# A gated unit with a quantised second product: block 11 of the first batch moves to the seven-product scheme, in a new order of steps

## The chip, the core and the metric

The kernel runs on one core of one Trainium2 chip. The core has four compute engines, each with its own queue that it works off in order: TensorE (PE, matrix products; PEld is its weight load), VectorE (DVE), ScalarE (ACT) and GpSimd (POOL). SyncE (SP) computes nothing here; it issues the transfers between the chip's memory (DRAM) and the on-chip memory, and also waits for its next instruction's inputs in order. The results of TensorE go to banks of PSUM, where ScalarE and VectorE read them. The metric is the device time of one launch in microseconds (us); the time before is 719.89 us, the median of three runs from 719.88 to 720.88.

## The reference

Four sequences of 1024 tokens with 512 features. Each is normalised, scaled by a row that depends on a condition vector, and goes through a gated unit whose down weights and hidden values are quantised.

```python
scale = cond @ norm_w.T + 1.0
ms = jnp.mean(x * x, axis=-1, keepdims=True)
h = x * (scale[:, None, :] * jax.lax.rsqrt(ms + EPS))
u = h @ up_w.T                       # 512 -> 2 x 2048
val, gate = jnp.split(u, 2, axis=-1)
h = val * jax.nn.gelu(gate, approximate=False)
hq = act_quant(h)                    # per token, 127 steps
wq = weight_quant(down_w)            # -1, 0, 1 times one scale
y = hq @ wq.T
return y + x
```

## The kernel before

A batch is one sequence: two halves of 512 tokens. The 2048 hidden rows are 16 blocks of 128. The first matrix product is made in fp16 from a high and a low part of each operand. For one block there are two ways to make it.

**The plain way.** `half_gate` and `half_value` (through `plain`, whose matmuls are at L715) make gate and value of one half of the tokens, 12 matmuls each over 512 columns. A block takes four such products, 48 matmuls. `half_gelu` (ScalarE, L761) and `half_out` (VectorE, L771) follow for each half.

**The seven-product way.** A class `Slot` makes a block's two halves of tokens at once from sums and differences of quarters of the weights and of the tokens: seven products (`product`, L700) of six matmuls each. Its steps have numbers in the written order: 0 first product, 1 its copy to a second bank (ScalarE, L807), 2 fourth product, 3 its copy (ScalarE, L815), 4 fifth product, 5 its copy (ScalarE, L822), 6 second product, 7 its gelu (ScalarE, L829), 8 third product, 9 its output (VectorE, L835), 10 gate product, 11 a sum (VectorE, L843), 12 the second gelu (ScalarE, L846), 13 value product, 14 a sum (VectorE, L852), 15 the second output (VectorE, L855). Products 0, 4, 8 and 13 collect in one bank A, 6 in the bank B, 2 and 10 in one bank E. There are two banks A, one B and two E; the plain gates take A or B, the plain values E. A bank is taken again when what reads it has run.

Batches 1 to 3 use the seven-product way throughout, with weights that the first batch prepares and spills to DRAM (`s_dram`). In the first batch the blocks below `FAST` go the plain way and those from `FAST` on (12 to 15 before) the other one.

**What the first batch prepares for a block j.** `w_load` brings the weights (SyncE, L306), `w_range` takes the mean of their size on ScalarE (L322), `w_factor` makes a power of two of it (VectorE, L332 to L342), `w_scale` scales (ScalarE, L372). `rows_high` and `rows_low` split the rows into fp16 parts (ScalarE L398, VectorE L402), and `rows_turn` brings them, transposed by the transfer itself, to the place from which TensorE loads them (SyncE, L406). `s_sum` (L436), `s_high` (ScalarE, L453) and `s_low` (L457) make the sums of quarters; a third number 1 in the name of an s_sum, or of an s_low after the part's number, puts it on VectorE, else it runs on GpSimd. `s_spill` (SyncE, L469) stores the parts in DRAM for the later batches. For a block from `FAST` on, the first batch needs the sums itself: they are made in a tile `s_rows`, and `s_turn` (SyncE, L475) brings them transposed to the place that products 2, 4 (s_turn.j.0) and 10, 13 (s_turn.j.1) read; `rows_turn` then brings three parts of the rows and not four.

**The order.** The whole first batch after the first half block is one text, `FIRST_BATCH`, which `take` reads from left to right; each name is a step, with its block and its part. It fixes the order on every engine's queue and on that of SyncE. A step waits for what it reads and for the space that it writes, and everything behind it on its queue waits too. Steps on different queues that stand next to each other in the text need not run at the same time. Besides the steps above it holds the tokens of the second batch (`t_` steps; `t_turn` L675), the loads of the down weights (`d_` steps), the four turns of the first tokens (`turn`), the maxima for the quantisation (`max`, VectorE), and steps for the condition's rows (`c_`; `c_over`, `c_spread`, `c_rows` and `d_spread` have a small matmul each).

The batches after it have their own loops and their own planner (`Filler`), which the change does not touch.

Of the kernel before, what the change touches and what calls it, by code (L numbers as in the profile page):

```python
# [51 lines left out]
def glu_quant_kernel(  # L52
# [18 lines left out]
    NJ = FF // P  # L71
# [71 lines left out]
    FAST = NJ - 4  # L143
# [1216 lines left out]
    def take(steps):  # L1360
# [10 lines left out]
        w_scale.3.0 o_whole.1.0.1 out.1.0 gate.1.1 rows_high.3 rows_low.3 d_sum.4 w_load.5 gelu.0.1
        s_high.0.1 value.1.1 s_sum.1.1.1 s_high.1.0 s_low.0.1.1 s_spill.0.0 out.0.1 d_sum.5 w_factor.4
        s_sum.1.3.1 w_load.10 s_low.1.0.1 d_sum.6 gate.2.0 rows_turn.3 o_WHOLE.3.2.1 s_high.1.1 w_range.5
        s_low.1.1 w_scale.4.0 s_sum.2.0.1 value.2.0 s_sum.2.2.1 t_square.0.1 s_sum.2.3.1 w_factor.5 gelu.1.1
        o_sum.0 w_scale.4.1 s_spill.1.0 rows_high.4 out.1.1 d_load.0 c_over gate.2.1 s_spill.2.1 w_scale.5.0
        w_gain.2 o_sum.1 gelu.2.0 w_gain.4 o_sum.2 o_high.1 value.2.1 d_sum.7 out.2.0 s_sum.2.1.1 rows_low.4
        rows_turn.4 s_high.2.0 w_scale.5.1 s_low.2.0.1 gate.3.0 o_high.3 o_low.1 o_high.2 w_load.6 o_sum.3
        d_sum.2 value.3.0 o_low.3 rows_high.5 t_square.0.0 rows_low.5 rows_turn.5 gelu.2.1 gate.3.1 gelu.3.0
        out.2.1 gelu.3.1 out.3.0 c_range s_spill.2.0 w_load.9 value.3.1 o_low.2 w_load.7 s_spill.3.1
        w_range.6 w_load.11 s_sum.3.0.1 s_sum.3.2 d_load.1 s_high.2.1 w_factor.6 w_scale.6.1 t_root.0  # L1380
        c_spread c_rows gate.4.0 c_copy s_low.2.1.1 s_sum.3.3 w_scale.6.0 s_sum.3.1.1 out.3.1 rows_high.6
        rows_low.6 rows_turn.6 s_high.3.0 s_low.3.0 value.4.0 d_sum.3 max.0.0.0 w_range.7 max.1.0.0
        s_sum.4.0 gelu.4.0 gate.4.1 w_factor.7 o_high.0 s_sum.4.1 s_sum.4.2.1 s_spill.4.1 w_scale.7.0
        o_low.0 w_load.8 w_scale.7.1 c_store value.4.1 out.4.0 rows_high.7 max.1.0.1 s_high.3.1 rows_low.7
        rows_turn.7 d_sum.0 gate.5.0 s_high.4.0 s_low.4.0 s_low.3.1.1 max.0.1.0 d_sum.1 c_undo gelu.4.1
# [443 lines left out]
```

## Time and profile before

The profile is one execution on the chip. Times are in us from its first instruction; a busy time is the union of an engine's instructions.

| | |
|---|---|
| median of the runs shown | 719.89 us (719.88 to 720.88, three runs) |
| span of the profiled execution | 718.6 us (1.29 less than the median) |
| TensorE busy | 712.7 us, 3664 matmuls |
| VectorE, ScalarE, GpSimd busy | 587.3, 423.6, 135.9 us |
| the order's first matmul, block 11, slot 12, the second batch begin | 21.1, 132.4, 142.8, 176.5 us |

A row of a timeline gives the start, the length, the engine, the line, what is written and read, and the number of instructions merged. A row of groups gives the line, engine and operation, the count, the busy time in us, the mean of one in ns, and the idle time of the engine just before, with what ended it. A row of stretches gives the length, then each engine's busy time with its number of instructions (TensorE, weight loads, VectorE, ScalarE, GpSimd), the granted clock of TensorE, the mean busy share of the 16 DMA engines and the GB/s moved. The modelled end of a matmul overlaps the start of the next one; the start of one to that of the next is the pace.

### The profile page before, as it was taken

Reading aid. Unit: us, or ns where it says so; the run is one execution under the profiler, and the core shown is the slowest. Engines: PE = TensorE matmul, PEld = TensorE weight load, DVE = VectorE, ACT = ScalarE, POOL = GpSimd, SP = SyncE. Lnnn points to the kernel's source line nnn. Section 1 sums busy time; section 2 is a strip of 40 time slices with the busy share of each in tenths; the row PEclk is TensorE's granted clock in tenths of the full one; section 3 lists DMA queues with packets and bytes.
Section 4 is the critical chain, followed back from the end, with each engine's and each line's share of the span. In section 5 each row is a group of like instructions: output and inputs, shape, how many; then the busy total and the mean of one; then the engine's idle time right before and its main releaser. Section 6 shows DMA issues by size and latency. Waiting matters only on the chain.

```text
span 718.6 us, 10218 instructions
## 1 busy us (share of the span) xinstructions
PE 712.7 (99%) x3664; PEld 359.6 (50%) x3664; DVE 587.3 (82%) x880; ACT 423.6 (59%) x703; POOL 135.9 (19%) x143
## 2 busy tenths in 40 slices
PE   8999999999999999999999999999999999999998
PEld 4544444444444446665444445665444444445854
DVE  7898897889898879896788868876688888755896
ACT  6998865786568784544335676544334665333463
POOL 1703233330100215340100031460020000000120
DMA  7799988998985556777745547775945444443253
GB/s 255 255 273 299 259 211 242 261 226 210 252 207 118 130 160 140 217 173 172 152 100 116 132 100 195 162 181 160 203 105 102 102 102 102 100 95 99 104 171 122
DMA packets 227060, 121.57 MB, mean 169 GB/s; under 512 B 188969, under 2 KB 198461, under 8 KB 227010
## 3 DMA queue, kind: packets, MB, share of 16 engines
q1 hardware_dynamic: 226858, 120.80, 67.6%
q8 instruction: 28, 0.46, 0.3%
q14 instruction: 22, 0.18, 0.1%
q10 hardware_dynamic: 152, 0.13, 0.1%
HBM read 52.71 MB, written 23.09 MB: 105 GB/s over the span
## 4 chain that ended last, share of the span: by engine, by line
PE 99%; ACT 0%; DVE 0%; issue 0%
PE A L700 37%; PE E L700 19%; PE B L700 9%; PE po L1064 9%; PE pg L715 8%; PE pv L715 8%; PE po_end L1016 4%; PE pz L1181 1%; PE ptx L1165 1%; PE pv L786 0%; PE po_B L1064 0%; PE pg L786 0%; PE pw L382 0%; PE po_E L1064 0%; PE po_A L1064 0%; PE pc L211 0%
## 5 line engine op out<-in xcount | busy, mean ns | idle before, releaser
L700 PEld LDWEIGHTS <-SXY 128*128 128x128 f16 x2100 | 205.5, 98 | 240.5
L700 PE MATMUL A<-R,SXY 128*128 128x512 f16 x1146 | 264.8, 379 | 0.0
L700 PE MATMUL E<-R,SXY 128*128 128x512 f16 x582 | 141.5, 379 | 0.0
L835 DVE SCALAR_TENSOR_TENSOR H<-A,sg,t 128x512 f32<-128x512 f32 x52 | 39.0, 750 | 69.6 <-PE A L700 69.4
L987 DVE TENSOR_TENSOR H<-H,am 128x1024 f32<-128x1024 f32 x64 | 76.0, 1214 | 0.0
L846 ACT ACTIVATE t<-t,sg 128x512 f32<-128x512 f32 x52 | 37.5, 720 | 63.3 <-DVE t L843 63.3
L700 PE MATMUL B<-R,SXY 128*128 128x512 f16 x300 | 72.9, 379 | 0.0
L906 DVE TENSOR_REDUCE gm<-H 128x512 f32<-128x1024 f32 x56 | 69.1, 1233 | 1.0
L829 ACT ACTIVATE t<-B,sg 128x512 f32<-128x512 f32 x52 | 35.7, 687 | 37.8 <-PE B L700 37.8
L922 POOL PARTITION_ALL_REDUCE am<-R x8 | 14.3, 1793 | 229.6 <-DVE R L908 229.6
L715 PEld LDWEIGHTS <-SXY 128*128 128x128 f16 x342 | 33.4, 98 | 40.3 <-DVE SXY L424 0.4
L1064 PE MATMUL po<-wd,R 128*128 128x256 fp8e4 x416 | 52.4, 273 | 0.0
L822 ACT COPY t<-A 128x512 f32<-128x512 f32 x52 | 30.2, 580 | 37.5 <-PE A L700 37.1
L815 ACT COPY v<-E 128x512 f32<-128x512 f32 x52 | 30.4, 585 | 32.1 <-PE E L700 30.2
L1064 PEld LDWEIGHTS <-R 128*128 128x128 bf16 (+1 forms) x448 | 43.8, 98 | 8.9
L807 ACT COPY B<-A 128x512 f32<-128x512 f32 x52 | 29.7, 572 | 31.2 <-PE A L700 30.6
L855 DVE SCALAR_TENSOR_TENSOR H<-v,sg,t 128x512 f32<-128x512 f32 x52 | 40.8, 785 | 6.6 <-ACT t L846 6.6
L852 DVE TENSOR_TENSOR v<-A,v 128x512 f32<-128x512 f32 x52 | 35.6, 685 | 9.2 <-PE A L700 8.0
L995 ACT ACTIVATE H<-H 128x1024 f32<-128x1024 f32 x38 | 39.9, 1050 | 5.2 <-DVE H L987 5.2
L715 PE MATMUL pg<-R,SXY 128*128 128x512 f16 x180 | 41.4, 379 | 0.0
L908 DVE TENSOR_TENSOR R<-R,gm 128x512 f32<-128x512 f32 x56 | 40.3, 720 | 1.1
L999 ACT ACTIVATE R<-H 128x1024 bf16<-128x1024 f32 x38 | 40.1, 1056 | 1.0
(236 smaller groups left out, 947.3 us busy)
## 6 DMA issues: line engine op xcount, KB each, us to landing
SXY<-s_dram SPq DMA_DIRECT2D x46, 256.0 KB, 3.1
H<-in_L_cond_up_w_dram SPq DMA_DIRECT2D x13, 512.0 KB, 3.9
SXY<-s_dram SPq DMA_DIRECT2D x46, 128.0 KB, 3.4
s_dram<-SXY SPq DMA_DIRECT2D x15, 384.0 KB, 4.9
xr<-in_x_dram SPq DMA_DIRECT2D x19, 256.0 KB, 3.0
out_dram<-xr SPq DMA_DIRECT2D x19, 256.0 KB, 2.6
H<-in_x_dram SPq DMA_DIRECT2D x8, 512.0 KB, 7.7
R<-in_L_cond_down_w_dram SPq DMA_DIRECT2D x8, 512.0 KB
```

The lines of the kernel that those rows point to most:

```text
L700: PE.matmul(o, s[:, w, k, :], operand(g // NJ, c, l, k), start=start and n == 0, stop=stop and n == len(TERMS) - 1, skip_group_check=True,)
L715: PE.matmul(ps, a[k // 2][:, w, k % 2, :], XP[:, l, k, h * TOK : (h + 1) * TOK], start=n == 0, stop=n == len(terms) - 1,)
L829: ACT.activation(self.t1, self.B, AF.Gelu, scale=gain(self.g, 1))
L835: DVE.scalar_tensor_tensor(h_half(self.g, 0), self.A, gain(self.g, 0), self.t1, ALU.mult, ALU.mult)
L846: ACT.activation(self.t2, self.t2, AF.Gelu, scale=gain(self.g, 1))
L855: DVE.scalar_tensor_tensor(h_half(self.g, 1), self.v, gain(self.g, 0), self.t2, ALU.mult, ALU.mult)
L906: DVE.tensor_reduce(gm[0], v, AX.X, ALU.max, apply_absolute_value=True)
L908: return [largest, lambda: DVE.tensor_tensor(m, m, gm[0], ALU.max)]
L987: DVE.tensor_tensor(v, v, r.to_broadcast([P, 2, TOK]), ALU.mult)
L995: ACT.activation(v, v, AF.Copy, bias=MAGIC)
L999: ACT.activation(q, by_tile(v), AF.Copy, bias=-MAGIC)
L1064: PE.matmul(po, w[:, j], m, start=start and j == 0, stop=stop and j == n - 1, skip_group_check=True,)
```

## The change

`FAST` goes from 12 to 11, so block 11 gets the steps of a slot: `gate.11`, `value.11`, `gelu.11` and `out.11` (two each) leave the order, and `slot.11.0` to `slot.11.15`, `s_turn.11.0` and `s_turn.11.1` come in. Its sums are made in `s_rows` (two and two parts, not three and one) and spilled from there, and its rows are split and turned in three parts.

The order as a whole is written anew. The set of steps is otherwise the same, but for the engine of s_sum, s_low and t_sum steps: of the 64 s_sum, 36 stay on VectorE though not the same ones; of the 32 s_low, 11 are on VectorE after 20; of the 16 t_sum, 8 after 11. TensorE's products of the plain blocks change places in a few spots (gate.4.0 ahead of gate.3.1, gate.5.1 ahead of gate.5.0, gate.9.1 ahead of gate.9.0, gate.10.1 ahead of value.10.0).

The core of the diff, with the stretches that matter below:

```diff
@@ -140,7 +140,7 @@
     A21 = R[:, 0, 6144 : 6144 + 768].bitcast(F16).rearrange("p (n w f) -> p n w f", n=3, w=2)

-    FAST = NJ - 4
+    FAST = NJ - 5
...
@@ -1363,75 +1363,73 @@
     FIRST_BATCH = """
-        w_load.3 d_load.2 t_load.0 d_load.6 d_load.4 s_sum.0.1 o_whole.0.0.0 gate.1.0 x_scale.6 w_range.3
-        x_scale.7 gelu.1.0 o_whole.2.2.0 turn.4 w_range.2 turn.5 w_load.4 turn.6 turn.7 d_load.7 x_high.0
...
-        s_spill.5.2 out.6.0 rows_turn.10 t_square.1.1 gate.8.0 max.2.0.0 rows_high.11 t_root.1 gelu.7.1
-        s_sum.8.0.1 s_high.7.1 s_sum.8.2.1 s_spill.6.2 s_high.8.0 s_low.7.1.1 s_sum.8.3 s_spill.6.0
...
-        rows_high.12 t_low.1.0 t_turn.1.0 gelu.9.1 gate.10.0 rows_low.12 t_high.1.1 t_square.2.0 t_low.1.1
-        s_high.10.1 s_sum.11.1.1 rows_turn.12 s_sum.11.2.1 s_high.11.0 s_low.10.1 value.10.0 out.9.1
-        s_sum.11.3 gelu.10.0 t_turn.1.1 w_range.13 max.3.0.1 w_load.14 s_low.11.0.1 s_sum.12.1 t_square.2.1
-        s_spill.12.1 gate.10.1 w_factor.13 w_scale.13.1 out.10.0 s_high.11.1 s_spill.10.1 t_root.2
-        s_low.11.1.1 w_scale.13.0 s_spill.11.0 rows_high.13 value.10.1 t_scale.2.1 w_range.14 s_sum.12.0.1
-        s_sum.12.2.1 s_sum.12.3.1 w_load.15 s_high.12.0 rows_low.13 s_high.12.1 gate.11.0 rows_turn.13
-        gelu.10.1 s_low.12.0.1 s_sum.13.0 t_high.2.1 w_factor.14 out.10.1 s_spill.12.0 t_scale.2.0
-        t_high.2.0 t_sum.2.1 value.11.0 s_turn.12.0 max.2.1.0 w_scale.14.0 s_sum.13.2 gelu.11.0 s_low.12.1.1
-        w_scale.14.1 t_sum.2.0 out.11.0 gate.11.1 s_turn.12.1 gelu.11.1 s_sum.13.1 s_spill.12.2 s_spill.10.0
-        t_sum.2.2.1 t_load.3 s_sum.13.3 value.11.1 rows_high.14 rows_low.14 s_high.13.0 s_low.13.0.1
-        slot.12.0 slot.12.1 t_sum.2.3.1 s_spill.13.0 max.2.1.1 s_turn.13.0 slot.12.2 s_sum.14.0.1 t_high.2.2
-        t_low.2.2 rows_turn.14 slot.12.4 s_high.13.1 s_low.13.1 slot.12.3 slot.12.6 slot.12.5 max.3.1.0
-        w_range.15 slot.12.13 t_low.2.0 s_spill.13.2 w_gain.14 s_turn.13.1 s_sum.14.2.1 t_square.3.1
-        out.11.1 slot.13.0 s_high.14.0 s_sum.14.3 slot.12.14 t_turn.2.0 slot.12.7 w_factor.15 s_sum.14.1
-        slot.13.2 slot.13.1 s_low.14.0.1 t_square.3.0 s_spill.14.0 slot.13.6 w_scale.15.0 t_root.3
...
+        s_sum.0.1 w_load.3 d_load.2 x_scale.7 x_scale.6 gate.1.0 w_range.2 turn.7 turn.4 turn.6 turn.5 w_range.3
+        w_factor.3 w_factor.2 d_load.4 value.1.0 gelu.1.0 d_load.5 x_high.1 o_whole.0.0.0 x_high.2 x_high.0
+        s_sum.0.0.1 x_low.2 x_low.0 d_load.6 x_low.1 d_load.7 x_high.3 o_whole.2.2.0 s_sum.0.2 x_low.3 s_sum.0.3
+        w_scale.3.0 s_high.0.1 w_scale.2.1 gate.0.1 w_scale.2.0 s_high.0.0 s_low.0.0 w_load.4 rows_high.2
+        rows_low.2 s_sum.1.0.1 gelu.0.1 w_scale.3.1 rows_high.3 t_load.0 d_sum.4 d_load.3 c_largest rows_turn.2
...
+        w_factor.11 gate.8.0 s_low.7.0 out.7.0 s_sum.7.3 t_low.0.1 t_square.1.1 s_high.7.1 s_sum.8.1.1
+        s_sum.8.0.1 s_spill.6.0 s_spill.9.1 out.6.0 s_spill.5.2 s_sum.8.2.1 w_scale.11.1 s_low.7.1 s_high.8.0
+        w_scale.11.0 s_sum.8.3 s_low.8.0.1 s_sum.9.1 rows_high.11 rows_turn.10 s_sum.9.0.1 s_sum.9.2.1
+        s_high.8.1 s_spill.7.0 value.8.0 gate.8.1 t_turn.0.1 s_spill.6.2 value.8.1 out.7.1 max.2.0.1 s_low.8.1
...
+        t_sum.1.0.1 w_range.12 t_high.1.0 rows_turn.11 out.8.0 value.9.0 t_sum.1.1 s_spill.8.0 out.8.1
+        s_sum.10.0.1 t_low.1.0 s_low.9.1.1 w_factor.12 w_scale.12.1 t_sum.1.2 w_gain.10 s_sum.10.2 s_sum.10.3
+        t_sum.1.3.1 t_high.1.2 w_load.13 s_high.10.0 s_spill.11.1 w_scale.12.0 t_low.1.2 s_high.10.1
+        s_low.10.0.1 s_sum.11.0.1 t_turn.1.2 gelu.9.0 rows_high.12 value.9.1 s_sum.11.2 w_gain.12 rows_low.12
+        s_sum.11.1.1 t_high.1.1 gate.10.0 gelu.9.1 s_high.11.0 w_range.13 s_low.11.0 t_square.2.0 s_spill.10.1
+        t_turn.1.0 t_low.1.1 gate.10.1 out.9.1 s_low.10.1.1 rows_turn.12 s_sum.11.3 s_sum.12.0.1 value.10.0
+        gelu.10.0 out.9.0 max.3.0.1 max.2.1.0 s_high.11.1 w_factor.13 w_scale.13.1 w_load.14 w_scale.13.0
+        s_sum.12.2 t_square.2.1 s_spill.11.0 rows_high.13 gelu.10.1 s_low.11.1.1 value.10.1 s_turn.11.1 t_root.2
+        w_range.14 slot.11.0 s_sum.12.1 s_spill.11.2 slot.11.1 s_sum.12.3.1 rows_low.13 s_high.12.0 s_turn.11.0
+        w_load.15 s_high.12.1 w_factor.14 slot.11.2 t_scale.2.1 t_turn.1.1 s_low.12.0 slot.11.6 slot.11.3
+        out.10.0 s_spill.12.1 slot.11.4 slot.11.10 rows_turn.13 slot.11.5 t_high.2.1 s_spill.12.0 s_sum.13.0.1
+        s_low.12.1 s_turn.12.0 s_sum.13.2.1 w_scale.14.1 max.2.1.1 w_scale.14.0 t_sum.2.0.1 slot.11.13
+        t_scale.2.0 slot.11.7 out.10.1 slot.11.14 s_spill.12.2 s_sum.13.3.1 t_sum.2.2 slot.12.0 s_high.13.0
+        slot.12.2 s_turn.12.1 t_load.3 t_sum.2.3.1 slot.12.1 rows_high.14 s_sum.13.1.1 s_high.13.1 s_spill.10.0
+        s_low.13.0 rows_low.14 slot.12.4 s_sum.14.0.1 w_gain.14 s_spill.13.0 t_sum.2.1 s_low.13.1 s_turn.13.0
+        slot.12.3 slot.11.11 s_turn.13.1 slot.12.6 slot.11.8 t_high.2.2 slot.11.12 t_low.2.2 slot.11.9 slot.12.5
+        s_sum.14.2.1 w_range.15 slot.12.13 rows_turn.14 t_square.3.1 slot.11.15 max.3.1.0 t_high.2.0 slot.12.7
+        slot.13.0 w_factor.15 slot.13.2 s_high.14.0 slot.13.1 w_scale.15.1 s_low.14.0 slot.12.14 t_square.3.0
...
     """
```

More of the change, by code (lines that the diff above doesn't have):

```diff
@@ L1371, in glu_quant_kernel @@
[L1371 to L1385, printed above, removed]
@@ L1391, in glu_quant_kernel @@
-        value.6.0 t_high.0.1 s_spill.4.2 out.5.1 s_spill.4.0 s_spill.8.1 t_scale.0.0 t_sum.0.2 s_sum.6.1.1
-        gate.6.1 w_range.10 t_sum.0.1 t_load.1 t_sum.0.3.1 w_gain.8 w_factor.10 gelu.6.0 s_high.6.0
-        value.6.1 rows_turn.9 gelu.5.0 t_high.0.2 out.5.0 gelu.6.1 t_low.0.2 gate.7.0 t_high.0.0
-        w_scale.10.1 out.6.1 w_scale.10.0 s_low.6.0.1 s_sum.7.0 s_high.5.1 s_spill.5.0 rows_high.10
-        t_turn.0.2 value.7.0 s_sum.7.1.1 s_low.5.1.1 s_sum.6.3 s_high.6.1 t_low.0.0 rows_low.10 t_turn.0.0
@@ L1435, in glu_quant_kernel @@
+        max.6.0.0 t_turn.3.1 slot.14.15 max.6.0.1 max.6.1.0 max.6.1.1
     """
```

69 lines of the change are left out of this document (39 added, 30 removed).

## The prediction

> **What bounds the kernel now.** I read the page first: the span, the engines' busy time and the chain of work that ended last.
>
> ```profile
> span 718.6 us, 10218 instructions
> PE 712.7 (99%) x3664; PEld 359.6 (50%) x3664; DVE 587.3 (82%) x880; ACT 423.6 (59%) x703; POOL 135.9 (19%) x143
> PE 99%; ACT 0%; DVE 0%; issue 0%
> ```
>
> TensorE is busy for 712.7 of 718.6 us and the chain is TensorE alone. So a part of the change is worth what it takes off TensorE's own list, less the gaps that it opens there. Where the 5.9 us of gaps lie now, the view by stretches tells (TensorE's busy time stands first after the length):
>
> ```profile
> 0.00:21.00 21.00, 18.37 (x90) 9.87 (x91) 16.80 (x78) 14.32 (x33) 5.21 (x10) 1.00 0.77 263
> 28.00:132.00 104.00, 104.00 (x486) 47.38 (x484) 88.26 (x157) 84.56 (x162) 33.81 (x36) 1.00 0.94 251
> 132.00:143.00 11.00, 11.00 (x52) 5.00 (x51) 8.62 (x15) 7.60 (x15) 4.83 (x6) 1.00 1.02 308
> 143.00:176.00 33.00, 33.00 (x154) 14.98 (x153) 28.75 (x46) 24.40 (x43) 8.56 (x10) 1.00 1.03 219
> 176.00:710.00 534.00, 534.00 (x2813) 275.07 (x2812) 434.90 (x568) 286.63 (x440) 77.47 (x77) 1.00 0.60 142
> 710.00:718.60 8.60, 5.36 (x36) 3.30 (x34) 3.13 (x5) 0.00 (x0) 0.00 (x0) 1.00 0.46 174
> ```
>
> There are 2.63 us of gaps before 21 us, where the written order's first matmul stands, and 3.24 us after 710 us; from 28 to 710 us there is none, at a granted clock of 1.00. The first batch has nothing to win but matmuls, and whatever comes late there is lost at once.
>
> **What is removed from TensorE.** The timeline of TensorE over block 11 and the start of slot 12, in the order before:
>
> ```profile
> 132.43 2.75 PE L715 MATMUL pg<-R 128*128 128x512 f16 x12
> 142.79 1.46 PE L700 MATMUL A<-R,SXY 128*128 128x512 f16 x6
> 144.09 1.46 PE L700 MATMUL E<-wd,SXY 128*128 128x512 f16 x6
> 145.38 1.46 PE L700 MATMUL A<-wd,SXY 128*128 128x512 f16 x6
> ```
>
> Block 11 begins at 132.43 and slot 12 at 142.79: four plain products of 12 matmuls in 10.36 us, 0.2158 us a matmul. A product of the seven-product scheme starts 1.295 us after the one before it (144.09 to 145.38), six matmuls at the same pace. Block 11 needs 48 matmuls now and 7 x 6 = 42 afterwards. Term: 6 x 0.2158 = **-1.295 us**. The order keeps its four turns and its four small matmul steps, so nothing else of TensorE's work changes. With no gap the span is 718.6 - 1.295 = 717.3; the median of the runs shown is 719.89, 1.29 above the span, and 719.89 - 1.295 = 718.6.
>
> **What is added to the other engines.** The groups of 21 to 183 us (the mean of one in ns stands after the comma):
>
> ```profile
> L761 ACT ACTIVATE g<-pg,sg 128x512 f32<-128x512 f32 x23 | 15.5, 677 | 4.2 <-PE pg L715 4.1
> L771 DVE SCALAR_TENSOR_TENSOR H<-g,sg,pv 128x512 f32<-128x512 f32 x20 | 14.8, 742 | 5.4 <-ACT g L761 2.8 <-PE pv L715 2.5
> L807 ACT COPY B<-A 128x512 f32<-128x512 f32 x5 | 2.9, 570 | 3.4 <-PE A L700 3.4
> L815 ACT COPY v<-E 128x512 f32<-128x512 f32 x5 | 2.9, 587 | 1.5 <-DVE H L855 1.5
> L822 ACT COPY t<-A 128x512 f32<-128x512 f32 x4 | 2.3, 580 | 2.3 <-PE A L700 2.3
> L829 ACT ACTIVATE t<-B,sg 128x512 f32<-128x512 f32 x5 | 3.4, 685 | 1.6 <-PE B L700 1.6
> L835 DVE SCALAR_TENSOR_TENSOR H<-A,sg,t 128x512 f32<-128x512 f32 x4 | 3.0, 746 | 1.4 <-PE A L700 1.4
> L843 DVE TENSOR_TENSOR t<-E,t 128x512 f32<-128x512 f32 x3 | 2.1, 684 | 0.0
> L846 ACT ACTIVATE t<-t,sg 128x512 f32<-128x512 f32 x3 | 2.2, 722 | 1.5 <-DVE t L843 1.5
> L852 DVE TENSOR_TENSOR v<-A,v 128x512 f32<-128x512 f32 x4 | 2.7, 686 | 0.1
> L855 DVE SCALAR_TENSOR_TENSOR H<-v,sg,t 128x512 f32<-128x512 f32 x3 | 2.2, 744 | 0.0
> ```
>
> ScalarE: five instructions of a slot (0.570 + 0.587 + 0.580 + 0.685 + 0.722 = 3.14 us) for two gelus (1.35): +1.8 us. VectorE: four (0.746 + 0.684 + 0.686 + 0.744 = 2.86) for two outs (1.48): +1.4 us, and the new order takes net nine s_low and three t_sum off it and gives them to GpSimd. ScalarE is busy for 24.4 and VectorE for 28.75 of the 33 us from 143 to 176, so I cost the totals at nothing: TensorE's 44 us from slot 11's start hide them. If that cover is gone, a late copy stops TensorE for its own 0.57 us, because one bank B and two banks each of A and E hold all products.
>
> The queue of SyncE gets two transposes more (s_turn.11.0 and .1), and rows_turn.11 brings three parts in place of four; the spills of block 11 carry the same bytes, two and two parts in place of three and one. What such a transpose costs, and when those of block 12 came:
>
> ```profile
> L475 SPq DMA_TRANSPOSE SXY<-s_rows x6: 1232/1254/1288, 136.9 to 168.0; - x6
> DMA to landing us min/median/max: 3.3/3.3/3.4
> 136.90 3.44 SPq L475 DMA_TRANSPOSE SXY<-s_rows x2
> 144.02 1.28 SPq L475 DMA_TRANSPOSE SXY<-s_rows  x1
> ```
>
> (1.25 us of the queue each, 3.3 us from issue to landing.) Costed at nothing while they land ahead of their products. So the sum hangs on due times, and the narrowest are those of slot 11's second product, slot.11.2: in the new order slot.11.0 stands where block 11 began, at 132.43, and slot.11.2 is due at 132.43 + 1.295 = 133.72. It waits for two things.
>
> First, a bank E: two values of slot 10 hold both, and out.10.0 on VectorE frees one. It is queued behind t_scale.2.1 and w_factor.14, and that waits for w_range.14 at the end of a row of eight steps on ScalarE from gelu.10.0 on. gate.10.0 starts four plain products before 132.43, at 122.07, and ends by 122.07 + 2.75 = 124.8.
>
> ```profile
> L372 ACT ACTIVATE H<-H,iv 128x512 f32<-128x512 f32 x28 | 19.2, 716 | 4.3 <-DVE iv L342 4.3
> L322 ACT ACTIVATE H<-H 128x512 f16<-128x512 f32 x26 | 16.1, 621 | 3.8 <-DMA H<-in_L_cond_up_w_dram 3.8
> L322 ACT ACTIVATION_READ_ACCUMULATOR H<-H 128x1 f32 x26 | 4.9, 190 | 0.0
> L398 ACT CAST H<-H 128x768 f16<-128x768 f32 x4 | 3.3, 830 | 0.1
> L453 ACT CAST s_rows<-H 128x512 f16<-128x512 f32 x8 | 4.8, 613 | 0.7 <-DVE H L436 0.7
> L621 DVE SCALAR_TENSOR_TENSOR xn<-xn,rs,sc 128x512 f32<-128x512 f32 x4 | 3.0, 746 | 0.0
> L332 DVE TENSOR_TENSOR undo<-wam,undo 128x2 int32<-128x2 int32 x13 | 3.7, 284 | 1.5 <-ACT H L322 1.5
> L334 DVE TENSOR_REDUCE sw<-undo 128x2 f32<-128x4 f32 x13 | 2.0, 157 | 0.4
> L342 DVE RECIPROCAL iv<-sw 128x2 f32<-128x2 f32 x14 | 2.3, 166 | 0.5
> L457 POOL TENSOR_TENSOR s_rows<-H,s_rows 128x512 f16<-128x512 f32 x3 | 4.4, 1481 | 12.5 <-ACT s_rows L453 12.5
> L457 DVE TENSOR_TENSOR s_rows<-H,s_rows 128x512 f16<-128x512 f32 x5 | 3.7, 746 | 1.0 <-ACT s_rows L453 1.0
> L436 POOL TENSOR_TENSOR H<-H 128x256 f32<-128x256 f32 x28 | 22.3, 800 | 48.4 <-issue 19.2 <-DVE undo L332 7.7 <-DVE H L436 7.1
> ```
>
> ScalarE: gelu 0.68, s_high.11.1 0.61, two w_scale 1.43, t_square (one pass and a read like those of L322) 0.81, rows_high.13 0.83, gelu.10.1 0.68, w_range.14 2 x 0.81 = 1.62: 6.66 us, so 131.5. Then on VectorE w_factor.14 0.61 (0.284 + 0.157 + 0.166), t_scale 0.75, out 0.74: 133.6. That is 0.1 us ahead of the due time, if ScalarE waits for nothing in between. Second, s_turn.11.0: s_low.11.1 follows s_high.11.1 (124.8 + 0.68 + 0.61 = 126.1) and takes 0.75 on VectorE, so 126.9 if VectorE is free; then the queue runs s_turn.11.1 (1.25), a spill (0.3 to 0.5) and s_turn.11.0, issued at 128.6 and landed at 131.9, 1.8 us early. The bounds: with neither late the gap is 0; if everything queued on ScalarE slips by one weight scaling (0.72), it is 0.6. A gain below 0 is excluded, since TensorE has no gap there to close. I take 0, to which both sums are nearest.
>
> By the same rows an s_low of such parts takes 1.48 us on GpSimd and 0.75 on VectorE, so a moved one reaches its transpose 0.7 us later; I cost that at nothing where the landing has more room. [...]
>
> Sum: -1.295 + 0 = **718.6 us**, a ratio of 0.9982.
>
> **Rivals.** *A late transfer at slot.11.2 (slower).* In the written order s_turn.11.0 stands behind slot.11.1 and s_high.12.0. In the order before, place and time agree: s_turn.13.0 stands just ahead of slot.12.2, and they start at 144.02 and 144.09. Read so, slot.11.1 starts no sooner than 132.43 + 1.46 = 133.89, s_high.12.0 0.57 later, and s_turn.11.0 lands at 134.46 + 3.3 = 137.8: a gap of 4.1 us, 718.6 + 4.1 = 722.7. It decides from a landing at 135.0 on (the gain is used up) and costs over 0.2% from 136.5 on. Against it: the new order is no timetable, since 26 steps stand between gate.8.0 and value.8.0 and none between value.8.0 and gate.8.1; only the order on each queue counts, and by that the sum above has it 1.8 us early.
>
> *Late at slot.12.2.* This product started at 144.09 and is due at 141.50 in the new order (seven products stand between 132.43 and it: 132.43 + 7 x 1.295). Its transpose s_turn.12.0 went out at 136.90 and would land at 140.2; two transposes more (2.5 us) ahead of it on the queue make that 142.7, 1.2 us late: 719.8. For it speaks a DMA share of 1.02 there; against it that the queue has room where t_turn.1.1 is placed later.
>
> [...]
>
> *More than the matmuls.* The transfers of the first 21 us are reordered too (t_load.0 goes behind four of d_load). If a tenth of the 2.63 us of gaps went, 718.3. Against it: TensorE's work before 21 us isn't part of the order.
>
> That the change doesn't do what it says is no rival: the list holds the sixteen steps of slot 11 and no gate or value of it.
>
> **How the numbers follow.** Forecast 0.46, late at slot.11.2 0.26, late at slot.12.2 0.13, GpSimd 0.05, more than the matmuls 0.10. A measurement of this kernel can tell about 0.2%, 1.44 us, from no change. The forecast's 1.295 us lies just inside, as do the third and fourth: within 0.2% 0.46 + 0.13 + 0.05 = 0.64; faster 0.10; slower 0.26. The range goes from 718.3 to 722.8: it takes in the forecast, both small losses and the price of the late transfer; the likeliest case's own range is 718.5 to 719.2 (a gap of 0 to 0.6).
>
> **What would show it.** Right: the page has 3658 matmuls, a span near 717.3 and no TensorE gap from 28 to 710 us; slot.11.0 starts at 132.4, slot.11.2 1.295 later; out.10.0 ends and s_turn.11.0 lands before that. Wrong: a gap of TensorE at its first product in bank E after 132 us, with VectorE as the releaser (the bank) or a transfer (the transpose); a gap before slot.12.2; or gaps before 132 us, where I checked no due time, and which would say that the new order costs more than slot 11 does.

## The result and the profile after

The changed kernel takes **732.23 us** (median of five runs, 731.78 to 732.93) against 719.89 (719.86 to 720.88) before: 1.017 times as long, with a 95% interval of 1.0157 to 1.0182. It is slower by 12.3 us; the forecast of 718.6 and its range (718.3 to 722.8) are both wrong. The page of the kernel after:

```profile
span 731.1 us, 10221 instructions
PE 714.6 (98%) x3658; PEld 359.2 (49%) x3658; DVE 593.1 (81%) x870; ACT 424.4 (58%) x706; POOL 160.6 (22%) x155
PE 73%; DMA 3%; ACT 3%; DVE 2%; POOL 2%; issue 2%; SPq 1%; POOLq 0%; ACTq 0%; DVEq 0%
```

The six matmuls are gone (3658). But the chain of work that ended last, TensorE alone before, now runs through transfers and every other engine: TensorE waits. GpSimd is busy for 24.7 us more, and VectorE for 5.8 us more although it runs ten instructions fewer.

By stretches, kernel after (the columns as before: length, TensorE, weight loads, VectorE, ScalarE, GpSimd, granted clock, DMA share, GB/s):

```profile
28.00:132.00 104.00, 101.67 (x473) 46.05 (x471) 88.40 (x145) 81.43 (x157) 49.16 (x43) 1.00 0.91 241
132.00:143.00 11.00, 7.43 (x29) 2.96 (x28) 5.82 (x12) 6.30 (x13) 4.39 (x5) 0.87 0.97 273
143.00:176.00 33.00, 30.17 (x136) 13.21 (x135) 28.00 (x39) 21.84 (x42) 15.62 (x16) 0.99 0.91 192
```

All three stretches were full before. Now 2.33, 3.57 and 2.83 us are idle, and the second ran at a clock of 0.87. What TensorE waited for over the whole span, kernel after (total, times, longest):

```profile
PE E L700 <- DMA R<-s_rows: 3.6, 1, 3.6
PE A L700 <- ACT t L822: 2.0, 3, 1.4
PE E L700 <- DVE t L843: 1.8, 1, 1.8
PE pz L1181 <- DVE eps L1111: 1.5, 1, 1.5
PE pv L715 <- DVE H L771: 1.3, 2, 1.1
PE pg L715 <- ACT g L761: 1.0, 1, 1.0
```

The fourth line is the first matmul of the kernel, 1.5 us as before. The others are new; they belong to eleven gaps of the first batch, from 41 to 197 us. Measured from the start of one product to the next less its own pace they come to 12.2 us (the modelled ends make them some 0.16 us shorter each in the views); with 1.6 us of half clock in this execution (last section) less 1.3 us of matmuls that is 12.5 us, the 731.1 - 718.6 of the two spans.

**The largest gap**, at slot.11.2. TensorE, kernel after:

```profile
135.20 1.46 PE L700 MATMUL A<-R 128*128 128x512 f16 x6
140.23 2.74 PE L700 MATMUL E<-wd,R 128*128 128x512 f16 x6 [3.57 <-DMA R<-s_rows]
```

The second product, due 1.295 us after 135.20, starts at 140.23, 3.74 us late. Its two conditions, in rows of SyncE's queue, of ScalarE and of VectorE, kernel after:

```profile
131.99 0.58 SPq L306 DMA_DIRECT2D H<-in_L_cond_up_w_dram  x1
133.18 1.49 SPq L475 DMA_TRANSPOSE R<-s_rows  x1
135.46 2.48 SPq L475 DMA_TRANSPOSE R<-s_rows  x1
```

```profile
136.88 0.63 ACT L322 ACTIVATE H<-H 128x512 f16<-128x512 f32 x1 [1.39 <-DMA H<-in_L_cond_up_w_dram]
```

```profile
139.38 0.74 DVE L771 SCALAR_TENSOR_TENSOR H<-g,sg,pv 128x512 f32<-128x512 f32 x1
```

The third row of the first fence is s_turn.11.0, issued at 135.46 (and landed at 140.18). The L322 row is w_range.14: ScalarE stood 1.39 us for w_load.14, issued at 131.99, and w_factor.14 and out.10.0 came behind it; out.10.0 ended at 139.38 + 0.74 = 140.12. Both conditions were late, to within 0.06 us of each other, and TensorE went on at 140.23.

**Smaller gaps**, at slots 14.0 and 14.2, show how long steps of VectorE reach TensorE. GpSimd, VectorE and TensorE, kernel after:

```profile
162.94 1.91 POOL L457 TENSOR_TENSOR s_rows<-H,s_rows 128x512 f16<-128x512 f32 x1 [0.76 <-ACT s_rows L453]
164.81 1.17 POOL L634 TENSOR_TENSOR xt<-xa 128x256 f32<-128x256 f32 x1
165.94 1.60 POOL L436 TENSOR_TENSOR H<-H 128x256 f32<-128x256 f32 x2
167.49 0.91 POOL L634 TENSOR_TENSOR xt<-xa,xt 128x256 f32<-128x256 f32 x1
```

```profile
163.75 1.65 DVE L621 SCALAR_TENSOR_TENSOR xa<-xa,rs,sc 128x512 f32<-128x512 f32 x1
165.32 0.74 DVE L835 SCALAR_TENSOR_TENSOR H<-A,sg,t 128x512 f32<-128x512 f32 x1
166.02 0.93 DVE L634 TENSOR_TENSOR xt<-xt,xa 128x256 f32<-128x256 f32 x1
166.87 0.95 DVE L634 TENSOR_TENSOR xt<-xa 128x256 f32<-128x256 f32 x1
167.74 0.94 DVE L436 TENSOR_TENSOR H<-H 128x256 f32<-128x256 f32 x1
168.60 0.68 DVE L843 TENSOR_TENSOR t<-E,t 128x512 f32<-128x512 f32 x1
```

```profile
166.11 1.46 PE L700 MATMUL A<-R 128*128 128x512 f16 x6 [0.31 <-DVE H L835]
169.34 1.46 PE L700 MATMUL E<-wd,R 128*128 128x512 f16 x6 [1.77 <-DVE t L843]
```

The L621 row takes 1.65 us where the step took 0.75 before; the three of 256 columns take 0.93 to 0.95 where such a step takes 0.42 alone (0.43 for L436 at 132.84 and 0.42 for L634 at 143.41, with GpSimd idle). Beside each of them GpSimd is reading. The stretch is 0.90 + 0.51 + 0.53 + 0.52 = 2.5 us, and the two TensorE gaps behind the L835 and L843 rows are 0.47 and 1.93.

### The profile page after: what moved, and what is told of

The parts are those of the page before. It is cut to its first block, busy times and chain, and to the rows that moved or that the text cites. A ratio compares the mean times of both kernels' runs of the same rounds, so it can differ in the third digit from the quotient of the medians.

```text
span 731.1 us, 10221 instructions
## 1 busy us (share of the span) xinstructions
PE 714.6 (98%) x3658; PEld 359.2 (49%) x3658; DVE 593.1 (81%) x870; ACT 424.4 (58%) x706; POOL 160.6 (22%) x155
## 4 chain that ended last, share of the span: by engine, by line
PE 73%; DMA 3%; ACT 3%; DVE 2%; POOL 2%; issue 2%; SPq 1%; POOLq 0%; ACTq 0%; DVEq 0%
PE A L700 34%; PE E L700 17%; PE po L1064 9%; PE B L700 9%; PE po_end L1016 4%; DMA H<-in_L_cond_down_w_dram 1%; DMA dn<-in_L_cond_down_w_dram 1%; DMA R<-s_rows 1%; DMA H<-in_L_cond_up_w_dram 1%; POOL H L436 0%; POOL s_rows L457 0%; PE po_B L1064 0%; DVE gm L906 0%; ACT tn L557 0%; POOL xt L634 0%
## 5 line engine op out<-in xcount | busy, mean ns | idle before, releaser
L835 DVE SCALAR_TENSOR_TENSOR H<-A,sg,t 128x512 f32<-128x512 f32 x53 | 39.7, 749 | 68.8 <-PE A L700 67.9
L908 DVE TENSOR_TENSOR R<-R,gm 128x512 f32<-128x512 f32 x56 | 42.1, 751 | 1.1
L575 POOL TENSOR_SCALAR ssq<-ssq 128x2 f32<-128x2 f32 x12 | 4.2, 354 | 172.6 <-ACT xt L605 123.3
```

Of the source, the lines that this page charges most:

```text
L835: DVE.scalar_tensor_tensor(h_half(self.g, 0), self.A, gain(self.g, 0), self.t1, ALU.mult, ALU.mult)
L908: return [largest, lambda: DVE.tensor_tensor(m, m, gm[0], ALU.max)]
```

## The experiments

Times are medians; each has a ratio to runs of the kernel before on the same chip, with its 95% interval. Differences between versions are taken from the ratios, times 720 us: the changed kernel loses 12.2. "New order" is that of the changed kernel.

**The order and the scheme apart.** e1: the new order, block 11 plain.

```
-    FAST = NJ - 5
+    FAST = NJ - 4
...
- slot.11.0 ... slot.11.2 slot.11.6 ... slot.11.4 ... slot.11.13 ...
+ gate.11.0 ... value.11.0 ... gate.11.1 ... value.11.1 ...
```

> The new order with block 11 left in the plain scheme (48 matmuls, no transposing transfers of its own; its two gates and values stand where slot 11's products stood). If the order costs the time: the small gaps ahead of 132 us (3.0 us in the changed kernel) and behind 143 us (5.5 us, less what 1.3 us more of matmuls absorb) stay, and value.11.0 still waits some 2 us for bank E from out.10.0; 726 to 730 us. If slot 11's own transfers and banks cost it: the gaps around 132 to 143 us vanish and the rest with them, 719.5 to 721 us.

733.71 us, ratio 1.0187 (1.0172 to 1.0202), 13.5 us lost. The order alone loses it all; slot 11 isn't needed for the loss. That is beyond both ranges, but on the side of the order. It is 1.2 us more than in the changed kernel, about the price of six matmuls, but the two intervals overlap and some gaps lie elsewhere, so this doesn't measure the matmuls.

e2: the old order with slot 11's steps in place of the gates, gelus, values and outs of block 11.

```
-    FAST = NJ - 4
+    FAST = NJ - 5
...
- gate.11.0 ... value.11.0 ... gate.11.1 ... value.11.1 ... slot.12.0
+ slot.11.0 slot.11.1 slot.11.2 ... slot.11.6 slot.11.3 slot.11.4 ... slot.11.10 slot.11.5 ... slot.11.13 slot.11.7
+ ... slot.11.14 slot.12.0 ... slot.11.8 slot.11.11 ... slot.12.2
```

> The old order with block 11 in the seven-product scheme, its steps put in by hand where its gate and value stood; s_turn.11.0 goes on the queue right behind w_load.14 and s_turn.11.1 right behind s_low.11.1.1. If the order costs the time: all of the six matmuls' 1.3 us is gained, 718.4 to 719.2 us. If the scheme itself costs it (its transposes land after their due times of 133.7 and 137.6 us whatever the order): a gap of 2 us or more at slot.11.2 or slot.11.10, 721 to 725 us.

721.71 us, 1.0019 (1.0009 to 1.0029). In this version s_sum.12.1 stands ahead of s_high.11.1 and overwrites a sum of block 11, so the values of that block are not the reference's; the instructions are the same. The time lies in the second range, but not for its reason: no gap of 2 us, four small ones (1.44, 0.70, 0.53 and 0.71 us, the first two behind late transposes). What the scheme is worth is taken up at the end.

**The local gap.** e3 moves both things that slot.11.2 waited for, e10 only the bank's.

```
- s_turn.11.1 ... s_spill.11.2 ... s_turn.11.0 ... w_factor.14 slot.11.2 t_scale.2.1 ... out.10.0
+ s_turn.11.0 s_turn.11.1 ... s_spill.11.2 ... out.10.0 w_factor.14 slot.11.2 t_scale.2.1
```

> The changed kernel with the two things that slot.11.2 waited for moved ahead: s_turn.11.0 in front of s_turn.11.1 on the transfer queue, out.10.0 in front of w_factor.14 on VectorE. If the 3.7 us gap and the 1.6 us at half clock behind it are local: both go, less what becomes due next, 727 to 729 us. If the stages behind are late anyway and only inherit the gap (slack made by the gap is what keeps them in time): the time stays within 1 us of 732.2.

729.75 us, 1.0133 (1.0118 to 1.0148): 2.7 us back, somewhat less than expected. The gap shrinks from 3.74 to 1.65 us and the half clock goes in the profiled execution (a granted clock of 1.00 from 126 to 150 us), but the gap at slot.12.13 grows from 0.44 to 1.39 and one of 0.55 opens at slot.12.2.

> The changed kernel with out.10.0 alone moved ahead of w_factor.14 and t_scale.2.1 on VectorE. In the changed kernel slot.11.2 waited for two things that were late together, out.10.0 (ended at 140.12 us) and the transposed sums (landed at 140.18). If both conditions hold it: the time stays, 731.5 to 732.5 us. If bank E alone held it and the transfer only looked so: 2 us or more come back, 728 to 730 us.

730.04 us, 1.0139 (1.0126 to 1.0153): 2.2 us back with one condition moved, so the expectation that both held it falls as a statement about the time. The gap at slot.11.2 is then 1.94 us, on the transpose alone. In the profiled execution the half clock is gone too (1.00 from 126 to 150 us): a gap shorter by 1.8 us, 1.6 us of clock, and 0.9 us lost again at slot.12.13, slot.15.13 and gate.10.0. Of its four runs two have a mean clock of 0.998 again (last section).

**The engines.** e4: the new order, each s_sum, s_low and t_sum on its old engine. e12: the old order with block 11 plain, and the new engines. In both only the last number of 58 names changes, for example:

```
- s_low.7.0.1 ... t_sum.1.2.1 ... s_sum.9.3.1 ... s_sum.13.0
+ s_low.7.0 ... t_sum.1.2 ... s_sum.9.3 ... s_sum.13.0.1
```

> The changed kernel's order with every s_sum, s_low and t_sum on the engine that it had before (GpSimd 9 s_low and 3 t_sum fewer). If GpSimd's longer work and its meeting VectorE make the batch late: the gaps shrink by half or more, 723 to 728 us. If the order of the steps on the queues is what is late, and the engines are not: 731 us or more.

740.94 us, 1.0283 (1.0267 to 1.0298): 8.1 us worse than the changed kernel. In that form my theory of an overloaded GpSimd fell here: in this order, giving the steps back to VectorE makes the batch later still. (Its profile has two stretches of half clock where the changed kernel has one, and a mean granted clock of 0.995 for 0.997.)

> The kernel before, its order and its plain block 11 untouched; only the engine of 58 of the s_sum, s_low and t_sum steps is that of the changed kernel (GpSimd gets 9 s_low and 3 t_sum more). The prediction took this at nothing. If that holds: 720 to 721 us. If GpSimd's longer steps (1.3 to 2.1 us where VectorE takes 0.4 to 1.0) delay the transposes behind them: gaps of several us in all, 723 to 728 us.

724.43 us, 1.0057 (1.0040 to 1.0073): 4.1 us lost, with nothing but engines changed. The prediction had this at nothing. By the profile two gaps make it, 0.62 us at 57.1 and 2.07 us at 77.8 (the small matmul of d_spread, behind a late VectorE), and half clock behind the second, some 1.7 us (a granted clock of 0.96 from 60 to 100 us); from 132 us on TensorE is full:

```profile
28.00:132.00 104.00, 101.63 (x466) 45.64 (x464) 88.41 (x141) 80.84 (x154) 44.47 (x41) 0.98 0.87 239
```

The groups of VectorE's s_sum from 21 to 195 us, in the kernel before, and in e12:

```profile
L436 DVE TENSOR_TENSOR H<-H 128x256 f32<-128x256 f32 x36 | 15.8, 445 | 1.3 <-POOL SXY L457 0.4 <-POOL H L436 0.4
```

```profile
L436 DVE TENSOR_TENSOR H<-H 128x256 f32<-128x256 f32 x36 | 20.4, 571 | 7.7 <-POOL H L436 3.1 <-POOL s_rows L457 2.8 <-POOL SXY L457 1.4
```

The count is the same, 36, and each takes 571 ns for 445. To sum this up I took every VectorE step of the first batch after 20 us and subtracted the shortest length that this kind of step has in any of the runs. The rest, here called the excess, is 10.8 us before (195 steps, 139.9 us in all) and 19.9 in e12 (183 steps, 141.0): twelve steps fewer, and VectorE is about as busy as before (by the stretches from 28 to 176 us, 125.6 us before and 125.9 in e12). The changed kernel has 22.4 (185 steps, 145.2), e4 has 19.2 (197 steps, 149.6), the most VectorE time of all and the longest run. The sum depends on the choice of steps: over all VectorE instructions that begin from 20 to 195 us, with kinds by operation and shape alone, it is 12.7 before, 24.2 in e12, 24.4 in the changed kernel, 20.5 in e4. So only differences of several us count. In the old order, then, VectorE pays back by longer steps what GpSimd takes over. In the new order it does so only in part: from e4 to the changed kernel VectorE is busy 4.4 us less, and the time is 8.1 us shorter.

**The halves.** e6: old order up to gate.10.0 (about 122 us), new one behind it; e7 the mirror. Both have slot 11.

```
- s_sum.0.1 w_load.3 d_load.2 x_scale.7 ... t_high.1.1 gate.10.0
+ w_load.3 d_load.2 t_load.0 d_load.6 ... gelu.9.1 gate.10.0
...
```

> The steps up to gate.10.0 (about 122 us) in the old order, the rest in the new one, block 11 in the seven-product scheme. If the new order is late by its own make behind 122 us: the gap at slot.11.2 (3.7 us and 1.6 us of half clock) and most of the 5.5 us behind it stay, 727 to 730 us. If it only inherits what went late ahead of 122 us (GpSimd's chain, w_load.12): the gap at slot.11.2 goes and the time is 719 to 723 us.

> The mirror: the steps up to gate.10.0 in the new order, the rest in the old one with slot 11 put in by hand as in the run of the mended slot. If the lateness ahead of 122 us carries over: the 2 us of gaps up to there, and 2 us or more at slot.11.2, 723 to 728 us. If only the new order's own tail is late: those 2 us alone, 720 to 722 us.

e6: 728.0 us, 1.0104 (1.0089 to 1.0119). e7: 726.44, 1.0081 (1.0066 to 1.0097). The stretches before and behind 122 us (length, TensorE, clock, DMA share, GB/s), e6 and then e7:

```profile
28.00:122.00 94.00, 94.00 (x439) 1.00 0.92 257
122.00:200.00 78.00, 70.38 (x322) 1.00 0.97 225
```

```profile
28.00:122.00 94.00, 91.10 (x423) 1.00 0.89 238
122.00:200.00 78.00, 73.95 (x340) 1.00 1.03 241
```

Behind 122 us the new order is late by itself: with a full TensorE ahead of it (94.00 of 94.00) 7.62 us are idle. Ahead of 122 us it is late too (2.90 idle), and the old order behind it idles 4.05. Set against the slot in the old order (e5 below, 1.9 us lost), the halves lose 5.6 and 4.0 us more, 9.6 of the 10.4 between that and the changed kernel: each half of the order costs time. Neither "inherited" nor "its own tail alone" is right. How the idle time is split is less certain than these sums: the changed kernel has the same steps as e7 up to gate.10.0, and in its profile 1.32 us are idle ahead of 122 us; e7's profiled run was 1.6 us above its median.

**Moving the steps that TensorE waited for.** e8 moves twelve, e11 adds a second round.

```
- w_range.14 slot.11.0 s_sum.12.1 s_spill.11.2 slot.11.1
+ slot.11.0 s_sum.12.1 s_spill.11.2 slot.11.1 w_range.14
...
- t_scale.3.0 slot.12.9
+ slot.12.9 t_scale.3.0
...
- d_round.1 d_sign.0 slot.15.5
+ slot.15.5 d_round.1 d_sign.0
...
```

> The changed kernel with twelve steps moved a few places forward or back on their queues, each the step that a gap of TensorE waited for or one that stood in front of it: out.0.1 ahead of o_sum.0; w_gain.10 and gelu.9.0 behind t_high.1.0; s_turn.11.0 ahead of rows_turn.12; out.10.0 ahead of rows_low.13; w_range.14 behind slot.11.1; s_turn.12.0 ahead of rows_turn.13; slot.12.5 ahead of t_high.2.2; slot.12.9 ahead of t_scale.3.0; slot.12.11 ahead of t_sum.3.2.1; slot.13.14 ahead of max.3.1.1; slot.15.5 ahead of d_round.1. Engines and amounts of work stay. If the loss is urgent steps queued behind steps that are not: nearly all of 12.3 us comes back, 719 to 722 us. If the order overloads an engine (GpSimd's 24.7 us more, slower element work on VectorE): moving steps only moves the gaps, 727 us or more.

> The kernel with twelve steps moved, with a second round of moves, each for a gap that was left there: s_spill.10.0 right behind s_spill.10.1 (s_turn.13.0 waited until 152.3 us for it), w_load.14 ahead of rows_turn.12, slot.11.3 ahead of w_range.14 and s_high.12.0, slot.12.1 ahead of s_high.13.0, slot.11.9 ahead of t_low.2.2, slot.13.9 ahead of max.4.0.1. If the loss is nothing but urgent steps queued behind others: the gaps of 1.87, 1.13, 0.76, 1.02 and 2.10 us close, 721 to 724 us. If there is a load that place does not change (GpSimd's and VectorE's steps lengthen each other, the transfer queue is full): new gaps open in place of those, 727 to 731 us.

730.94 (1.0142 to 1.0170) and 730.1 us (1.0123 to 1.0153): 1.0 us (within the intervals of the two) and 2.3 us back where over 8 were expected, and my second theory, urgent steps behind others, fell. The gaps of the changed kernel did close or nearly so in e8 (value.2.1, gate.10.0, slot.11.2, slot.14.0, slot.14.2, slot.15.13); its waits show what opened in their place:

```profile
PE A L700 <- DVE H L835: 2.5, 2, 1.9
PE E L700 <- ACT v L815: 1.7, 1, 1.7
PE A L700 <- ACT t L822: 1.2, 1, 1.2
PE A L700 <- ACT B L807: 1.0, 1, 1.0
PE E L700 <- DMA SXY<-s_rows: 0.9, 1, 0.9
```

VectorE's excess stays at 22.1 and 22.3 us. My reading, which these two runs don't prove: with VectorE's time short by that much, moving steps chose which of them came late.

**GpSimd's reads.** e13: the changed kernel, but each first-batch s_sum, s_low and t_sum of GpSimd computes 8 columns and zeroes the rest by a memset, which writes only. e14 does it to the kernel before. e16: as e13, with the memset twice, for the length. In all three the rest of these sums is left out: 57 GpSimd steps in e13 and e16, 45 in e14 (not the 52 of its expectation). For s_low, in essence (s_sum and t_sum likewise):

```
- eng.tensor_tensor(s[:, :, 1], f, s[:, :, 0], ALU.subtract)
+ if eng is POOL:
+     eng.tensor_tensor(s[:, :, 1, :8], f[:, :, :8], s[:, :, 0, :8], ALU.subtract)
+     eng.memset(s[:, :, 1, 8:], 0.0)
```

> The changed kernel, order and engines untouched; each s_sum, s_low and t_sum that GpSimd runs in the first batch computes only the first 8 columns of each part and fills the rest with zeros by a memset, which reads nothing (so those sums are left out). If GpSimd's reading beside VectorE is what makes VectorE's steps long (22 us over their shortest in the first batch, against 11 us before) and these make the order late: VectorE's excess falls to 6 us or less and 8 us or more come back, 719 to 724 us. If the places of the steps on the queues are what is late, whatever the steps' length: 728 us or more.

> The control: the same replacement in the kernel before (52 GpSimd steps of the first batch compute 8 columns and zero the rest; those sums are left out). TensorE has no gap there to close, so both theories expect no gain, 719.5 to 720.8 us; a gain of over 1 us would mean that the replacement takes away something other than the gaps.

> The changed kernel with GpSimd's s_sum, s_low and t_sum of the first batch writing only, as before, but with the zeros written twice, so that each step is about as long as in the changed kernel (an s_sum 0.35 + 2 x 0.30 = 0.95 us against 0.96, an s_low of 512 columns 0.28 + 2 x 0.51 = 1.30 against 1.34). The sums are left out again. If what makes the order late is VectorE's steps being stretched by GpSimd's reads: VectorE's excess stays as low as with one memset and the time at 719.5 to 722 us. If it is the length of GpSimd's own steps (the transposes wait for them): 726 to 732 us again. In between, the two share it.

e13: **719.79 us**, 0.9992 (0.9983 to 1.0001), 12.8 us under the changed kernel. e14: 720.21, 0.9997 (0.9988 to 1.0006), nothing gained, as both theories had it. e16: **720.29 us**, 1.0003 (0.9994 to 1.0012), still 12.0 us under. Stretches and VectorE's s_sum (L428 in this version) in e16:

```profile
28.00:132.00 104.00, 103.88 (x485) 47.27 (x483) 80.43 (x150) 85.76 (x167) 50.08 (x122) 1.00 0.93 256
132.00:143.00 11.00, 11.00 (x53) 4.92 (x51) 6.35 (x14) 6.79 (x13) 5.20 (x15) 1.00 1.16 277
143.00:176.00 33.00, 32.78 (x153) 14.68 (x151) 28.13 (x44) 25.41 (x46) 13.23 (x37) 1.00 1.04 222
```

```profile
L428 DVE TENSOR_TENSOR H<-H 128x256 f32<-128x256 f32 x36 | 14.8, 418 | 2.7 <-POOL s_rows L428 1.7 <-POOL H L428 0.5
```

And the same group in the changed kernel:

```profile
L436 DVE TENSOR_TENSOR H<-H 128x256 f32<-128x256 f32 x36 | 20.1, 566 | 1.7 <-POOL s_rows L457 1.0 <-POOL H L436 0.4
```

GpSimd is as busy as in the changed kernel (50.08 + 5.20 + 13.23 = 68.5 us against 49.16 + 4.39 + 15.62 = 69.2), the order and the engines are the same, and TensorE is full but for 0.34 us. What is gone is the reading: VectorE's s_sum falls from 566 to 418 ns, its excess from 22.4 to 7.1 us (7.2 in e13, a little over the 6 expected). So how long GpSimd takes to its outputs doesn't make the batch late; its reading beside VectorE does, and the steps of VectorE that this stretches are measured. One other thing goes with the reading: a step lets go of its source sooner. In e16 five of VectorE's s_sum start 0.5 to 1.0 us before the end of the GpSimd step whose source they overwrite (one at 135.24, where the step read until 135.21 and ended at 136.22); in the changed kernel the same s_sum waits 0.95 us for that step to end. How much of the 12 us that is was not separated.

**The scheme where nothing is late.** e2's order was mended five times; each time steps ahead of its gaps were moved, as the expectations name them. The first and the last of these edits, e5's and e18's:

```
- s_sum.12.1 ... s_low.11.1.1
+ s_low.11.1.1 s_sum.12.1
...
- slot.12.7 slot.12.13 ... w_gain.14 ... t_square.3.1 ... slot.13.0 slot.13.1
+ slot.12.7 slot.12.13 ... slot.13.0 slot.13.1 w_gain.14 t_square.3.1
...
```

> The seven-product scheme for block 11 in the old order again, with s_sum.12.1 put behind s_low.11.1.1 (it overwrote a sum that slot 11 still had to read: the run before computed another result) and four steps moved: s_spill.10.1 and s_spill.10.0 go on the transfer queue some 3 us earlier (rows_turn.13 and s_turn.13.0 waited for them, and slot.12.2 and slot.13.2 for those, 1.4 and 0.7 us), slot.12.7 ahead of s_high.14.0, slot.15.5 ahead of d_sign.0. If these four are all that stood against the six matmuls' 1.3 us: 718.2 to 719.3 us. If late transfers come with the scheme wherever they are put: still a gap of 1 us or more at a slot product, 720.5 us or more.

> The slot in the old order once more, the transfer queue rearranged: s_spill.11.0 first (s_high.12.0 waited for its landing until 136.6 us and held slot.11.3 behind it, 0.74 us of gap), s_turn.12.0 ahead of s_spill.12.0 and rows_turn.13 (it was issued at 139.6 and landed 2.7 us after slot.12.2's due time, 1.26 us of gap), slot.11.3 still ahead of gelu.10.1. If the two gaps of the run before close: 718.3 to 719.6 us, 0.1 to 0.3 % under the kernel before. If the transfer queue is full there and the lateness only moves on: 720 to 722 us.

> The slot in the old order, the two gaps of the last version (0.72 us at slot.11.2, 0.50 at slot.13.2) taken up: s_turn.11.0 right behind w_load.14 and both ahead of t_turn.1.1; s_high.13.0 ahead of rows_high.14, s_low.13.0.1 ahead of t_sum.2.2.1, s_turn.13.0 ahead of s_spill.13.0. If they close: 1.2 us under that version's 720.65, 719.2 to 719.8 us, 0.1 % under the kernel before. If t_turn.1.1 or rows_high.14 is then late: 720.5 us or more.

> The slot in the old order with the three gaps of the last version taken up: slot.12.5 ahead of t_high.2.2 (0.74 us at slot.12.13), s_turn.13.0 ahead of t_load.3 and s_spill.12.0 ahead of s_turn.12.0 (0.63 us at slot.13.2), slot.12.7 behind w_range.15 and slot.13.1 ahead of s_high.14.0 (0.44 us at slot.13.6). If they close: 720.38 less 1.8, 718.5 to 719.3 us, the 1.3 us of the six matmuls under the kernel before. If s_turn.12.0 or w_gain.14 is then late: 720 us or more.

> The slot in the old order with the three gaps of the last version taken up (0.69 us at slot.13.6, 0.44 at slot.14.0, 0.58 at slot.14.2; the last two stand behind t_scale.3.0, which took 1.65 us beside GpSimd's s_low.14.1 where it takes 0.75 alone): slot.13.1 ahead of w_gain.14 and t_square.3.1, slot.12.9 ahead of t_sum.3.0.1, slot.12.11 right behind slot.12.10 and ahead of the gains. If the scheme is worth its six matmuls once nothing is late: 718.8 to 719.5 us, 0.13 to 0.2 % under the kernel before. If VectorE and GpSimd have no room for it in this batch: gaps open elsewhere, 720 us or more.

| | time, us | ratio (interval) | gaps of TensorE of 0.4 us or more in the profile |
|---|---|---|---|
| e5 | 722.03 | 1.0026 (1.0017 to 1.0034) | 0.74 slot.11.10, 1.26 slot.12.2 |
| e9 | 720.65 | 1.0006 (0.9997 to 1.0015) | 0.72 slot.11.2, 0.50 slot.13.2 |
| e15 | 720.38 | 1.0002 (0.9993 to 1.0010) | 0.74 slot.12.13, 0.63 slot.13.2, 0.44 slot.13.6 |
| e17 | 721.04 | 1.0006 (0.9998 to 1.0015) | 0.69 slot.13.6, 0.44 slot.14.0, 0.58 slot.14.2 |
| e18 | 720.83 | 1.0004 (0.9995 to 1.0013) | 0.45 slot.13.13, 1.26 slot.14.6 |

e9 and e18 closed the gaps that they were aimed at; in e5 the one at slot.12.2 stayed, in e15 that at slot.13.2 and in e17 that at slot.13.6. Each version has gaps of 1.2 to 2.0 us in all, about the 1.3 us of the six matmuls or more. Each forecast of 718.2 to 719.8 us missed. A list of gaps is from one execution, and the runs of one version lie 1.7 to 2.9 us apart. In e18, for one:

```profile
161.49 1.46 PE L700 MATMUL B<-R 128*128 128x512 f16 x6 [1.10 <-ACT B L807]
```

No version beat the kernel before. The best ones equal it within the interval.

## Why the prediction was wrong

**The step that failed** is the one that costs the engines' work at nothing: the text has "the new order takes net nine s_low and three t_sum off it and gives them to GpSimd" and then "I cost the totals at nothing: TensorE's 44 us from slot 11's start hide them". The runs put 4.1 us on that move in the old order (e12), 13.5 us on the move and the new order together without slot 11 (e1), and take 12.0 of 12.2 us away again when GpSimd's steps stop reading (e16). The move by itself isn't the whole: in the new order the kernel is slower without it (e4). What was costed at nothing is how the steps of the two engines meet in the new order. The totals of busy time were the wrong thing to look at, since they take the lengths of VectorE's steps as fixed: here these lengths grew by some 12 us.

**GpSimd, with a chance of 0.05,** was nearest to the cause, and its price was too small: one s_sum of GpSimd, 0.80 us, in the way of one step of VectorE. No run shows that term. What the runs showed in its place: VectorE's s_sum take 566 ns in the changed kernel, where GpSimd's steps read, and 418 in e16, where they only write; and with 57 GpSimd steps that can meet VectorE all over the batch its steps are over their shortest lengths by 11.6 us more than before (22.4 - 10.8). The rows that the prediction quotes are means (800 ns for GpSimd's s_sum, 445 for VectorE's). Rows of single steps of the kernel before would have shown more: of VectorE's 36 s_sum 34 take 0.40 to 0.43 us and two 0.89 to 0.90, and GpSimd's go from 0.72 to 1.59.

**The matmuls** were right in number, 3658, and in pace: products of the changed kernel follow one another at 1.295 us where nothing is late. That the slot nets nothing in the old order (e9 to e18) was not foreseen: there the six matmuls are gone and small gaps give their time back.

**The added copies** of slot 11 cost at most little: with GpSimd only writing, they are in place and the kernel is at 720.3.

**The due times at slot.11.2** named the right two conditions and missed both by over 6 us: out.10.0 ended at 140.12 (133.6 in the sum), the transpose landed at 140.18 (131.9), while slot.11.0 itself was only 2.8 us late (135.20 for 132.43). The sum held "if ScalarE waits for nothing in between", and it did wait, 1.85 us for w_factor.13 of VectorE ahead of w_scale.13 (at 132.24) and 1.39 us for w_load.14. That transfer went out at 131.99; in the kernel before:

```profile
128.44 0.53 SPq L306 DMA_DIRECT2D H<-in_L_cond_up_w_dram  x1
```

The transpose was priced by the wrong row, too. The row quoted, 1.25 us, is that of the six that go to SXY; slot 11's go to R, as two of the kernel before do, and these stand in the same view, one at 1.30 us and one at 2.67:

```profile
L475 SPq DMA_TRANSPOSE R<-s_rows x2: 1301/1985/2669, 152.2 to 159.6; - x2
```

**The rival of the late transfer** gave 4.1 us of gap and 3.74 were measured, but that is under a third of the loss, and e6 has a gap of 3.27 us there, on the bank, with a full TensorE ahead of it. The half clock behind the gap was not thought of. **Late at slot.12.2** did not happen in the changed kernel; it did (1.44 us) in e2. **Gaps before 132 us**, which the prediction listed as what would make it wrong and did not check, were 2.33 us.

**What stays open.** e12 and the changed kernel have nearly the same excess (19.9 and 22.4 us) and lose 4.1 and 12.2 us; e4 has less (19.2) and loses 20.4. So the excess alone doesn't give the loss. Which of VectorE's stretched steps TensorE feels depends on the order; which single places make the difference was not isolated. e4 was not run with GpSimd only writing. Nor was it tried whether the same order with GpSimd's steps at other times would keep VectorE short.

## What to carry to other kernels

Work moved from a fairly busy VectorE to an idle GpSimd wasn't free room here: VectorE's s_sum took 566 ns where GpSimd's steps read beside it and 418 where they only wrote, and twelve steps moved in the old order left VectorE about as busy as it was (125.6 us before, 125.9 in e12). It wasn't always a loss either: in the new order the same move saved 8.1 us. Price such a move with lengths measured beside the other engine, and over all the steps that can meet, not by one collision. And when gaps close and reopen elsewhere as steps are moved, stop moving: sum the lengths of the engine's steps against their shortest, and take the suspected cause away.

## What was not expected of the hardware

**Half clock behind a gap.** In the kernel after, right behind the 3.74 us gap (length, TensorE, clock, DMA share, GB/s):

```profile
140.00:144.00 4.00, 3.77 (x10) 0.57 1.06 285
```

Ten matmuls in 3.77 us, where the full pace makes 17.5: 7.5 x 0.2158 = 1.6 us lost on top of the gap. The length of the gap alone doesn't decide it. In e1 it came behind one of 2.26 us and in e12 behind one of 2.07, and in e6 it did not come behind one of 3.27; first e1, then e6:

```profile
126.00:130.00 4.00, 3.92 (x11) 0.59 1.07 269
```

```profile
137.00:141.00 4.00, 4.00 (x19) 1.00 1.07 285
```

What decides it besides, none of these rows shows. In the kernel after the half clock lasts about 3.4 us: a granted clock of 0.50 from 140.1 to 143.5.

Nor does the same kernel always get it. The mean granted clock of the changed kernel's five runs is 0.997, 1.000, 1.000, 0.998 and 0.998, and of e10's four 1.000, 1.000, 0.998 and 0.998, at 729.45, 729.48, 731.37 and 730.59 us; 3.4 us at half clock in 730 lower the mean by 0.002. So, as an estimate (half of these 3.4 us), some 1.7 us between single runs of such kernels can be the clock alone.

**A transpose's time on the queue** is no constant: s_turn.11.1 and s_turn.11.0 took 1.49 and 2.48 us to issue in the kernel after, against the 1.25 us of the sum. A busy DMA alone doesn't explain it: the DMA share is 0.97 from 132 to 143 us there and 1.02 in the kernel before, where the two in that stretch took 1.28 and 1.23 us. What does is open.
